# A graph network's last layer: sums transposed by VectorE in 32x32 blocks and put in place by transfers

## The chip, the core and the metric

The kernel runs on one core of a Trainium2 chip. The metric is the device time of one execution in microseconds (us). Before the change the median of three runs is 3499.28 us (3495.52 to 3499.89). A core has five engines that run their own instruction streams: TensorE (PE, with its weight loads shown apart as PEld), VectorE (DVE), ScalarE (ACT), GpSimd (POOL) and SyncE (SP). In this kernel SP only issues transfers; POOL and ACT issue some too. Sixteen DMA engines carry them out. Matmuls write to PSUM, eight banks of 2 KB for each of 128 partitions; the other engines work on PSUM and on the larger SBUF; transfers move data between SBUF and DRAM.

## The reference, cut to what matters

Four layers run on the same 3327 nodes with 512 features and one adjacency matrix. Each adds its result to its input and normalises the rows. The change touches the last one, an attention with 4 heads of 128 features:

```python
h = (x @ W).reshape(N, 4, 128).transpose(1, 0, 2)
si, sj = einsum('hnd,d->hn', h, a1), einsum('hnd,d->hn', h, a2)
e = leaky_relu(si[:, :, None] + sj[:, None, :], 0.2)
attn = softmax(where(adj > 0, e, -9e15), axis=-1)
y = elu(einsum('hij,hjd->hid', attn, h).transpose(1, 0, 2).reshape(N, 512))
x = layernorm(x + y)
```

## The kernel before

**Layout.** The nodes are padded to 26 tiles of 128 (`NT`), and split into two halves of 13 tiles, 1664 columns (`HALF`, `IW`). The attention layers (0, 2 and 3; layer 1 is a mean over neighbours) share the class `Layer`. `attention` (L478) runs eight units: two halves of target nodes by four slots `s`. In layers 0 and 2 a slot is two heads of 64 features (`HS` = 2), in the last layer, called L3, one head of 128 (`HS` = 1).

**One unit** (`unit`, L345) loops over the 26 tiles j of source nodes.

- L391: every second j, SP issues the load of `vj`, the scaled features of two tiles (128 KB). The pool has four buffers, so a load waits until PE has done with the fourth pair before it.
- L396: DVE makes `t`, 128x1664, the larger of two factors times the mask. The pool has three buffers in L3: DVE can be at most three j ahead of PE.
- L399: ACT makes `y`, a step function of `t`, in fp8.
- L405: PE adds `vj` transposed times `t` into the four PSUM banks `po`, which hold the unit's sums with features on partitions and nodes along the columns (`CUTS`: 448, 448, 384 and 384 columns). An f32 product shows as two rows of the trace.
- L365 (`den`): every second j, PE adds the products of `y` to the two banks `pd`, which hold denominators. In slot 0 there are twice as many.

**The end of a unit.** `po` has one set of banks, so the next unit's first products wait until the sums are out. DVE copies the first bank to `ob` in SBUF (L423), ACT the other three (L421). Then features must go from partitions to columns: `transposed` (L426) has PE transpose 128x128 blocks of `ob`, four at a time, into a bank `pt` (L429). That makes 13 transposes in four blocks. Without `final`, DVE (in L3) or ACT (elsewhere) copies `pt` to `hb` (L437, L435) and SP stores it to the DRAM tensor `hd` (L438). In half 1 of L3, `final` (L851) takes `pt`: in slots 0 and 1 DVE copies it to `g` in SBUF (L854); in slots 2 and 3 it goes through division, elu and addition at once, and in slot 3 into the statistics. At the end of slot 3 of half 0, and of slots 1, 2 and 3 of half 1, `pd` is copied too (L452, L453), and PE and DVE make the reciprocals `rec` (L455).

**Order.** `unit` returns the transposing steps as a list of jobs. The next unit takes one after each j (L410): two empty ones, then a block, an empty one, a block and so on. So PE does the transposes of one unit inside the next. A second list, `aside` (L801, `later`), gives further steps, one per j, in half 1: while slots 0 to 2 run, the rows of half 0 are loaded from `hd` (L126), divided (L180), put through elu (L185, L191, L192), normalised (L152 to L161) and stored to the output (L133). In slot 2 the first two slots of `g` are divided (L838, on DVE) and go through elu (L841, L846, L847); in slot 3 their statistics follow (L823). PE's order is that of the program. The order of DVE, ACT, POOL and SP is set by a scheduler that places instructions by modelled times and by dependencies.

Of the kernel before, what the change touches and what calls it, by code (L numbers as in the profile page):

```python
# [18 lines left out]
P = 128  # L19
# [13 lines left out]
def kernel(  # L33
# [10 lines left out]
    nc = tc.nc  # L44
# [6 lines left out]
    HALF = NT // 2  # L51
    FW = F // 2
    assert F == 512 and NT % 2 == 0 and N < NP and NT < 32
    IW = HALF * P
# [5 lines left out]
    QUADS = [(s, min(4, HALF - s)) for s in range(0, HALF, 4)]  # L60
# [53 lines left out]
    hd = dram.tile([NP, F], F32, name="hd")  # L114
# [108 lines left out]
    class Layer:  # L223
# [121 lines left out]
        def unit(self, pools, half, s, background, aside, final=None, ending=None):  # L345
            H, D, HS = self.H, self.D, self.HS
            tp, yp, vp, rp, sp, po_p = pools
            i0 = half * IW
# [6 lines left out]
            po = [po_p.tile([P, 512], F32, name=f"po{c}") for c in range(4)]  # L355
# [60 lines left out]
            den(NT - 2, late)  # L416

            ob = sp.tile([P, IW], F32, name="ob", bufs=1)
            for c, (a_, z) in enumerate(CUTS):
                if c:  # L420
                    nc.scalar.copy(ob[:, a_:z], po[c][:, :z - a_])  # L421
                else:
                    nc.vector.tensor_copy(ob[:, a_:z], po[c][:, :z - a_])  # L423
            t0 = half * HALF

            def transposed(s0, n):  # L426
                pt = qp.tile([P, 4, P], F32, name="pt", tag="q")
                for q in range(n):
                    nc.tensor.transpose(pt[:, q, :], ob[:, (s0 + q) * P:(s0 + q + 1) * P], ident)  # L429
                if final:  # L430
                    final(s, s0, n, pt)
                    return
                hb = sp.tile([P, 4, P], F32, name="hb")
                if HS == 2:
                    nc.scalar.copy(hb[:, :n], pt[:, :n])  # L435
                else:
                    nc.vector.tensor_copy(hb[:, :n], pt[:, :n])  # L437
                nc.sync.dma_start(out=hd[(t0 + s0) * P:(t0 + s0 + n) * P, s * P:(s + 1) * P]  # L438
                                  .rearrange("(t p) f -> p t f", p=P), in_=hb[:, :n])

            nothing = lambda: None
            jobs = [nothing, nothing]
            for s0, n in QUADS:
                jobs += [lambda s0=s0, n=n: transposed(s0, n), nothing]
            if s < NS - 1 and not (final and s > 0):
                return jobs

# [307 lines left out]
    def third(first):  # L755
        with tc.tile_pool(name="col3", bufs=1) as cp:
# [33 lines left out]
            with tc.tile_pool(name="f3", bufs=2) as fp, tc.tile_pool(name="f4", bufs=1) as gp:  # L790
                g = gp.tile([P, HALF, F], F32, name="g")
# [59 lines left out]
                def final(s, q0, n, pt):  # L851
                    qs = slice(q0, q0 + n)
                    if s < 2:
                        nc.vector.tensor_copy(g[:, qs, s * P:(s + 1) * P], pt[:, :n])  # L854
                        return
                    h = fp.tile([P, 4, P], F32, name="h", bufs=2)
                    nc.vector.tensor_tensor(h[:, :n], pt[:, :n], rec[:, HALF + q0:HALF + q0 + n, s:s + 1]
                                            .to_broadcast([P, n, P]), op=ALU.mult)
                    e = fp.tile([P, 4, P], F32, name="e")
                    nc.scalar.activation(e[:, :n], h[:, :n], AF.Exp)  # L860
                    y = g[:, qs, s * P:(s + 1) * P]
                    nc.vector.scalar_tensor_tensor(y, e[:, :n], 1.0, y, op0=ALU.min, op1=ALU.add)
                    nc.vector.scalar_tensor_tensor(y, h[:, :n], 0.0, y, op0=ALU.max, op1=ALU.add)
                    if s == NS - 1:
                        for q in range(q0, q0 + n):
                            nc.vector.bn_stats(out=st[:, q, 1, :], in_=g[:, q, FB:])
                            nc.vector.bn_aggr(out=mv[:, q, :], in_=st[:, q, :, :])

                L3.attention(lambda pool, half, s: [lambda: L3.prepare(fp, 1, "xr", 2), lambda: L3.cut(fp, 1, "e", 2)]
                             if (half, s) == (0, 0) else [], later=later, final=final)  # L870
                cut_ = min(8, HALF)
                for qs in (slice(0, cut_), slice(cut_, HALF)):
# [158 lines left out]
```

## Time and profile before

| | |
|---|---|
| median of three runs | 3499.28 us |
| the profiled execution | 3489.1 us |
| its span, first to last instruction | 3486.7 us |
| L3's attention, first product of its loop to last | 2766.9 to 3460 us of the span |
| 2786 to 3369: PE busy | 582.3 of 583.2 us |
| the same stretch: DVE, ACT busy | 413.0 and 402.2 us |
| mean granted clock of PE | 0.983 |
| one transpose (L429) | 273 ns |
| one t product (L396) | 1947 ns |
| one ob copy by DVE (L423), 128x448 | 617 ns |
| one pt copy by DVE (L437), 128x512 | 684 ns |

A line of the order of time gives the start, the length, the engine, the line of the kernel, the operation, output<-inputs, partitions x columns, and how many instructions are merged in it; in brackets the idle time before it and what ended that. Times inside the span are counted from its first instruction.

### The profile page before, as it was taken

The numbers are of one execution on the slowest core, as the hardware profiler recorded it, in microseconds if no ns is written. First come the engines' busy times: TensorE is split into PE (matmuls) and PEld (weight loads), VectorE is DVE, ScalarE is ACT, GpSimd is POOL, SyncE is SP. The second block draws the span as 40 slices with busy tenths as digits, with TensorE's granted clock in tenths as the row PEclk, the third lists the DMA queues.
The fourth block names the chain that finished last, engine by engine and source line by source line (L and its number), as shares of the span: only waits on it lengthen the run. The fifth ranks groups of instructions, "written<-read, shape, count | busy, mean of one in ns | idle before, by whom it ended". The sixth has DMA issues, their size and how long they took to land.

```text
span 3486.7 us, 48120 instructions
## 1 busy us (share of the span) xinstructions
PE 3325.6 (95%) x18873; PEld 1701.2 (49%) x18926; DVE 2694.9 (77%) x2759; ACT 2396.6 (69%) x2336; POOL 181.2 (5%) x289
## 2 busy tenths in 40 slices
PE   6899999999989999999998999999998999999997
PEld 5644444444444455555553444444446754555553
DVE  5599999999967644434439999999998756668886
ACT  1388989899953343433428999899998655558885
POOL 1000000000000111111110000000001000000000
PEclk9999999999999999999999999999999999999998
DMA  9535211101133432222221111111116511112211
GB/s 352 179 104 161 67 44 41 54 27 51 37 105 125 131 90 73 70 61 75 73 66 35 48 47 48 47 46 46 29 39 197 183 33 44 40 46 91 81 38 47
DMA packets 208452, 276.65 MB, mean 79 GB/s; under 512 B 19321, under 2 KB 140355, under 8 KB 208228
## 3 DMA queue, kind: packets, MB, share of 16 engines
q1 hardware_dynamic: 173622, 157.37, 14.1%
q0 software_dynamic: 22736, 89.80, 8.3%
q10 hardware_dynamic: 11870, 26.42, 2.4%
q8 instruction: 149, 2.44, 0.3%
q14 instruction: 75, 0.61, 0.1%
HBM read 204.92 MB, written 68.60 MB: 78 GB/s over the span
## 4 chain that ended last, share of the span: by engine, by line
PE 62%; issue 24%; DVE 6%; DMA 5%; ACT 3%; POOL 1%; POOLq 0%; DVEq 0%; SPq 0%; ACTq 0%
PE po L405 34%; PE acc L728 9%; PE pw L264 5%; PE pd L365 5%; DVE t L396 3%; PE pz L617 2%; PE pi L620 2%; DMA raw<-in_adjT_dram 2%; ACT y L399 1%; DMA cy<-ctd 1%; PE pt L429 1%; PE pk L696 1%; PE pt L253 1%; DVE kt L700 1%; PE pe L460 1%
## 5 line engine op out<-in xcount | busy, mean ns | idle before, releaser
L396 DVE SCALAR_TENSOR_TENSOR t<-rb,qc,mask 128x1664 f32<-128x1664 f32 x1040 | 1960.1, 1947 | 200.8 <-PE po L405 158.6
L399 ACT ACTIVATE y<-t,bi,sc 128x1664 fp8e4<-128x1664 f32 x1040 | 1771.7, 1766 | 341.4 <-PE pd L365 317.4
L405 PE MATMUL po<-t,vj 128*64 128x448 f32 (+3 forms) x8320 | 1939.5, 522 | 26.0 <-DVE t L396 24.6
L405 PEld LDWEIGHTS po<-t,vj 128*64 128x64 f32 (+1 forms) x8320 | 857.8, 148 | 977.7 <-issue 681.1
L728 PE MATMUL acc<-zs,kt 128*128 128x512 bf16 x1314 | 396.6, 381 | 1.9 <-issue 0.4
L264 PE MATMUL pw<-wsb,xT 128*128 128x264 f32 (+1 forms) x1248 | 299.3, 395 | 21.7 <-DVE vt L270 19.5
L688 ACT CAST pk<-cy 128x256 f32<-128x256 bf16 x338 | 124.0, 374 | 272.7 <-DVE kt L700 224.8
L728 PEld LDWEIGHTS <-kt 128*128 128x128 fp8e4 x2028 | 198.8, 98 | 229.6 <-issue 34.5
L264 PEld LDWEIGHTS pw<-wsb,xT 128*128 128x128 f32 x1248 | 238.9, 196 | 65.6 <-issue 18.8
L365 PE MATMUL pd<-y,sden 128*32 128x448 fp8e4 (+1 forms) x4160 | 259.8, 342 | 10.5 <-ACT y L399 10.5
L700 DVE SCALAR_TENSOR_TENSOR kt<-pk,mask 128x256 fp8e4<-128x256 f32 x338 | 140.9, 421 | 159.5 <-PE pk L696 158.9
L728 PE MATMUL acc<-zl,kt 128*128 128x512 bf16 x661 | 252.1, 381 | 1.1 <-DMA zl<-zd 0.5
L365 PEld LDWEIGHTS <-sden 128*32 128x32 bf16 x4160 | 117.8, 96 | 162.4 <-issue 139.8
L270 DVE TENSOR_TENSOR vt<-pw,dc 128x256 f32<-128x256 f32 x156 | 59.1, 418 | 98.1 <-ACT dc L265 93.5
L696 PE MATMUL pk<-mask,upto 128*128 128x256 fp8e4 x338 | 92.5, 274 | 21.1 <-ACT pk L688 20.0
L353 POOL DMA_DIRECT2D rb<-r x40 | 21.5, 539 | 1646.8 <-DVE t L396 1610.1
L268 ACT COPY fc<-pw 128x8 f32<-128x8 f32 (+1 forms) x156 | 22.8, 163 | 112.1 <-PE pw L264 101.8
L617 PE MATMUL pz<-wn,xT 128*128 128x512 f32 x208 | 95.0, 600 | 1.2 <-ACT xT L611 1.2
L620 PE MATMUL pi<-wl,xT 128*128 128x512 f32 x208 | 93.5, 592 | 0.0
L590 POOL DMA_DIRECT2D cy<-ctd x91 | 67.8, 745 | 400.2 <-ACT pk L688 273.5
L708 DVE SCALAR_TENSOR_TENSOR y<-acc,cnt,bnb 128x512 f32<-128x512 f32 x26 | 19.5, 751 | 85.1 <-PE acc L728 85.1
L524 DVE TENSOR_SCALAR mask<-raw 128x832 fp8e4<-128x832 int32 (+2 forms) x86 | 50.2, 592 | 45.0 <-DMA raw<-in_adjT_dram 44.4
(165 smaller groups left out, 1732.2 us busy)
## 6 DMA issues: line engine op xcount, KB each, us to landing
vj<-v SPq DMA_DIRECT2D x312, 128.0 KB
rb<-r POOLq DMA_DIRECT2D x40, 832.0 KB, 4.7
cy<-ctd POOLq DMA_DIRECT2D x78, 256.0 KB, 3.9
v<-vt SPq DMA_DIRECT2D x75, 256.0 KB
h<-hd SPq DMA_DIRECT2D x65, 256.0 KB
raw<-in_adjT_dram ACTq DMA_DIRECT2D x38, 416.0 KB
raw<-in_adjT_dram SPq DMA_DIRECT2D x37, 416.0 KB
hd<-hb SPq DMA_DIRECT2D x60, 256.0 KB
```

Source lines behind the costliest of these rows:

```text
L264: nc.tensor.matmul(pw[e][:, :FW + H], xT[:, c, :], wsb[:, c, e, :], start=c == 0, stop=c == FC - 1)
L365: nc.tensor.matmul(pd[c][32 * kk:32 * kk + 32, :w_], lhsT, rhs, start=(kk, c) not in seen, skip_group_check=final is not None, stop=last a ...
L396: nc.vector.scalar_tensor_tensor(t, rb[k], self.qc[:, j, h:h + 1], mask[:, j, i0:i0 + IW], op0=ALU.max, op1=ALU.mult)
L399: nc.scalar.activation(y, t, AF.Sigmoid, bias=self.bi[:, j, h:h + 1], scale=self.sc[:, j, h:h + 1], saturate=False)
L405: nc.tensor.matmul(po[c][k * D:(k + 1) * D, :z - a_], vj[:, j % 2, k * D:(k + 1) * D], ts[k][:, a_:z], start=j == 0, stop=j == NT - 1)
L590: nc.gpsimd.dma_start(out=cy[:, :n, :], in_=ctd[t:t + n, b * GW:(b + 1) * GW] .rearrange("(o t) i -> o t i", o=1).to_broadcast([P, n, GW]))
L617: nc.tensor.matmul(pz, xT[:, c, :], wn[:, c, :], start=c == 0, stop=c == FC - 1)
L620: nc.tensor.matmul(pi, xT[:, c, :], wl[:, c, :], start=c == 0, stop=c == FC - 1)
L688: nc.scalar.copy(pks[k % 2], carry[b, t // 4 * 4][:, t % 4, :])
L696: nc.tensor.matmul(pk, upto, mask[:, t, i0:i0 + GW], start=False, stop=True, skip_group_check=True)
L700: nc.vector.scalar_tensor_tensor(kt, pk, NEIGHBOURS, mask[:, t, i0:i0 + GW], op0=ALU.is_le, op1=ALU.mult, saturate=False)
L728: nc.tensor.matmul(acc, kts[t][:, s * P:(s + 1) * P], zs[:, t, c, :] if c < 2 else zl[:, t, :], start=t == 0 and c == 0, stop=t == NT - 1 ...
```

## The change

In L3 alone, in all units but slots 2 and 3 of half 1 (`by_dma`):

- DVE takes all four banks of `po` to `ob`, each with a transpose that works on squares of 32x32: within a square, rows and columns change places; the squares stay where they are. ACT has none of these copies.
- PE's 13 transposes, the copies out of `pt` and the stores of `hb` are gone from these units. Right after the four DVE transposes SP issues four transfers to `hd`, one for each group of 32 partitions. Each writes 32 features of 1664 nodes, in runs of 32 numbers (128 bytes), 1664 runs to a transfer.
- In half 1, slots 0 and 1, a job of the next unit (after its third j for slot 0, its fourth for slot 1) has SP load `g` from `hd`, in place of the DVE copies.

```diff
             ob = sp.tile([P, IW], F32, name="ob", bufs=1)
+            by_dma = HS == 1 and not (final and s > 1)
             for c, (a_, z) in enumerate(CUTS):
-                if c:
+                if by_dma:
+
+                    nc.vector.transpose(ob[:, a_:z], po[c][:, :z - a_])
+                elif c:
                     nc.scalar.copy(ob[:, a_:z], po[c][:, :z - a_])
                 else:
                     nc.vector.tensor_copy(ob[:, a_:z], po[c][:, :z - a_])
...
                 hb = sp.tile([P, 4, P], F32, name="hb")
-                if HS == 2:
-                    nc.scalar.copy(hb[:, :n], pt[:, :n])
-                else:
-                    nc.vector.tensor_copy(hb[:, :n], pt[:, :n])
+                nc.scalar.copy(hb[:, :n], pt[:, :n])
...
-            for s0, n in QUADS:
-                jobs += [lambda s0=s0, n=n: transposed(s0, n), nothing]
+            if by_dma:
+                for b in range(4):
+                    nc.sync.dma_start(out=hd[i0:i0 + IW, s * P + 32 * b:s * P + 32 * b + 32]
+                                      .rearrange("(q i) f -> i q f", i=32),
+                                      in_=ob[32 * b:32 * b + 32, :].rearrange("p (q f) -> p q f", f=32))
+                if final:
+                    jobs.append(lambda: final(s, 0, HALF, None))
+            else:
+                for s0, n in QUADS:
+                    jobs += [lambda s0=s0, n=n: transposed(s0, n), nothing]
...
                     if s < 2:
-                        nc.vector.tensor_copy(g[:, qs, s * P:(s + 1) * P], pt[:, :n])
+                        nc.sync.dma_start(out=g[:, qs, s * P:(s + 1) * P], in_=hd[HALF * P:, s * P:(s + 1) * P]
+                                          .rearrange("(q p) f -> p q f", p=P))
                         return
```

## The prediction, made before the changed kernel was run

> **What bounds the kernel now.** I read the busy times first, then the windows of the last layer, then its order of time on TensorE.
>
> ```profile
> PE 3325.6 (95%) x18873; PEld 1701.2 (49%) x18926; DVE 2694.9 (77%) x2759; ACT 2396.6 (69%) x2336; POOL 181.2 (5%) x289
> ```
>
> ```profile
> 2900.00:3000.00 100.00, 100.00 (x388) 50.19 (x386) 63.83 (x37) 55.79 (x35) 0.53 (x1) 1.00 0.13 38
> 3200.00:3300.00 100.00, 99.08 (x414) 51.41 (x407) 78.16 (x78) 87.41 (x72) 4.17 (x8) 1.00 0.27 84
> ```
>
> PE leads, but its share of the whole span would prove little. The windows of the changed stage (columns: stretch, its length, busy us of PE, PEld, DVE, ACT, POOL, clock, DMA share, GB/s) show PE without a gap while VectorE has 36 us of 100 free in half 0 and 22 in half 1. A busy PE need not be a PE at its peak, so I take the price of the transposes from the rhythm of the stream, not from their own durations. Half 0, slot 1, with and without a block of four transposes:
>
> ```profile
> 2872.58 0.56 PE L365 MATMUL pd<-y,sden 128*32 128x448 fp8e4 x8
> 2873.07 3.06 PE L405 MATMUL po<-t,vj 128*128 128x448 f32 x8
> 2875.96 0.60 PE L429 MATMUL pt<-ident,ob 128*128 128x128 f32 x4
> 2876.40 2.96 PE L405 MATMUL po<-t,vj 128*128 128x448 f32 x8
> 2879.29 0.56 PE L365 MATMUL pd<-y,sden 128*32 128x448 fp8e4 x8
> ...
> 2892.39 0.56 PE L365 MATMUL pd<-y,sden 128*32 128x448 fp8e4 x8
> 2892.88 5.86 PE L405 MATMUL po<-t,vj 128*128 128x448 f32 x16
> 2898.66 0.56 PE L365 MATMUL pd<-y,sden 128*32 128x448 fp8e4 x8
> ```
>
> From one pd group to the next (two values of j, a "pair") is 6.71 us with the block and 6.27 without. Four transposes cost the stream 0.44 us, 0.11 each, not the 0.273 that one lasts.
>
> **What goes from PE.** Six units lose 13 transposes each. They ran inside the following unit. In the four that are followed by slots 1, 2, 3 of half 0 and slot 1 of half 1: 3 x 0.44 + 0.12 (6.39 - 6.27, the single one) = 1.44 each, 5.8 together. Slot 0 of half 1 has pairs of 7.04 and 6.72 against 6.65: 3 x 0.39 + 0.07 = 1.24. Slot 2 of half 1 has 6.67 and 6.34 against 6.27: 1.27. Sum **8.3 us**, all on the path as long as nothing new stops PE.
>
> **What goes from the others.** ACT loses three ob copies per unit (3 x 0.478), DVE one ob copy (0.617) and the four copies out of pt (3 x 0.684 + 0.283). Neither bounds the stage; I count nothing.
>
> **What DVE gets: four transposes per unit.** The trace has no DVE transpose. Nearest row: the ob copy from the same PSUM bank, 128x448 in 0.617; 64 columns fewer at the slope of the pt copies ((683 - 283) ns / 384 columns) give 0.55. The four: 2.33 us. Upper end: a DVE operation that is slow per element, the reciprocal, 0.471 for 52 columns and 0.799 for 104, 6.3 ns a column: 2.8 and 2.4, together 10.5 us. Below the copy there is no reason to go. I take 2.33, since both move every element once. [...]
>
> Whether 2.33 is hidden is settled at the boundary of two units, here slot 1 to slot 2 of half 0:
>
> ```profile
> 2939.95 1.95 DVE L396 SCALAR_TENSOR_TENSOR t<-rb,qc,mask 128x1664 f32<-128x1664 f32 x1 [1.54 <-PE po L405]
> 2941.82 0.62 DVE L423 COPY ob<-po 128x448 f32<-128x448 f32 x1
> 2942.57 0.94 PE L365 MATMUL pd<-y,sden 128*32 128x448 fp8e4 x16
> 2942.68 0.48 ACT L421 COPY ob<-po 128x384 f32<-128x384 f32 x1 [0.17 <-PE po L405]
> 2943.44 4.89 PE L405 MATMUL po<-t,vj 128*128 128x448 f32 x13
> ```
>
> In the changed program's instruction order the transposes stand where the one copy stood, after the t of j=0 and j=1 of the next unit. So PE has 5.8 us of work in hand and DVE starts at 2941.8. PE wants the four banks back at 2943.44, 2944.2, 2945.0 and 2945.7; DVE is done with the last at 2944.15. The t of j=2, queued behind, is ready at 2946.1 and wanted at 2949.2. Cost nothing; the four may take 3.85 us before PE waits. After slot 0 the limit is 4.6, as the double set of pd products fills PE until 2860.77. At slot 0 to 1 of half 1 a t product now stands between the first and second transposes: 3197.2 + 0.62 + 1.87 + 1.7 = 3201.4, wanted by 3203.0. Nothing.
>
> Slot 1 to 2 of half 1 is different:
>
> ```profile
> 3279.96 1.95 DVE L396 SCALAR_TENSOR_TENSOR t<-rb,qc,mask 128x1664 f32<-128x1664 f32 x1 [0.33 <-PE po L405]
> 3281.83 0.69 DVE L191 SCALAR_TENSOR_TENSOR xr<-e,xr 128x512 f32<-128x512 f32 x1
> 3284.22 0.54 PE L365 MATMUL pd<-y,sden 128*32 128x448 fp8e4 x6 [0.92 <-ACT y L399]
> ```
>
> The scheduler now puts between that t (j=1) and the next: L180, L191, transpose, L192, L191, transpose, L192, two transposes, two db copies, two statistics, one aggregate. With 0.68 for each 512-column step (0.60 where they overlap): first transpose done 3283.7, second 3285.7, last 3287.5, next t (j=2) 3292.0. PE wants the banks from 3283.8: it waits 1.15 for the second, 0.45 for the third, and 0.8 for the t of j=2. That is 2.4, and the 0.92 that it waits there for ACT today falls inside it: **1.5 us lost**. Bounds: -0.9 (today's wait goes, none comes) to 4 (the e of L185 late too).
>
> At slot 2 to 3 the copy of the first bank now stands ahead of the t of j=0 and j=1. That t is ready 3.4 us after j=25 began, wanted after 2.89 + 0.87 = 3.8. Nothing, margin 0.4.
>
> **The transfers.** Each unit issues four scatters of 1664 packets of 128 B, 416 packets per DMA engine, in place of three of 512 and one of 128 packets of 512 B; two loads of g (1664 packets of 512 B) come new.
>
> ```profile
> q1 hardware_dynamic: 6045, 2.93, 10.1%
> ...
> hd<-hb SPq DMA_DIRECT2D x3, 256.0 KB
> ```
>
> In 2900 to 3000 a packet of 485 B took 0.101 x 100 x 16 / 6045 = 26.7 ns of an engine. For 128 B the lower end is by bytes, 7 ns. The upper end is 31, from the one row of tiny packets: the cb load, 3328 packets of 2 B, 208 per engine, landed 6.5 us after issue. I take 26.7: 11.1 us per unit.
>
> On SP's queue the scatters wait for the fourth transpose. In the changed order four vj loads of the next unit stand ahead of them; queued behind is its fifth, which PE releases 6.3 us into that unit and wants at 25.1. Landing takes 2.4 (the 128 KB xr load's), so the scatters must drain within 22 us, 53 ns a packet. Twice my price is hidden.
>
> [...]
>
> In half 1 the load of g waits on SP for the scatters to land. For slot 1: 3287.5 + 11.1 + 2.4, then 104 x 26.7 ns + 2.4: about 3306. DVE's first product on it (L838) now stands behind the t of j=10, which waits for PE to end j=7 at about 3314. Hidden by 8 us; without that cover DVE would hold PE up once the two t in hand, 6 us, are used.
>
> **Sum.** 8.3 - 1.5 = 6.8 us. The profiled execution took 3489.1 (span 3486.7 and 2.4 around it): it would be 3482.3. The shown runs have median 3499.28, 10 us above; I take the same 6.8 off it: **3492.5**. That is 0.19%, while 0.2% (7 us) is about what a measurement of this kernel can tell from no change. So the forecast lies on that line.
>
> **Rivals.** (1) No loss at the boundaries: L180 and L191 run earlier than I place them, ACT without its copies is in time. For it: 138 of DVE's waits in this stage are for PE. Against: DVE has least room there. 8.3 to 9.2 off: 3490 to 3491. (2) Half 1 gives most back: the scheduler's new order puts the t products late at slots 1 to 2 and 2 to 3, 3 to 6 us in all: 3495 to 3498, no change. (3) Slower, by the rate of the DVE transpose. Place: each boundary; price: whatever the four take over 3.85 us (4.6 after slot 0). At 10.5 us: 5.9 + 3 x 6.7 in plain boundaries, 6.5 and 10 in the two of half 1, 42 us: 3534. It decides from about 4.9 us for the four, where the six boundaries eat the 6.8. Against it: the copy row. (4) Slower, by the scatters: above 53 ns a packet the vj loads starve PE; at 65 ns 416 x 12 ns = 5 us in six units, 30 us: 3522. (5) It doesn't do what it says: PE is paced by something else and the freed slots stay empty: no change. Against: PE has no gap in 2900 to 3000.
>
> **Chances.** Forecast (4.5 to 8 off) 0.49, half of it beyond 7 us; (1) 0.20; (2) 0.13; (3) 0.08; (4) 0.07; (5) 0.03. Faster by over 0.2%: 0.245 + 0.20 = 0.45. Within: 0.245 + 0.13 + 0.03 = 0.40. Slower: 0.15. Range: 3486 is 9.2 off and 4 for the spread of the shown runs below their median; 3508 takes in (2) and the mild parts of (3) and (4), whose bounds beyond are left out with about 1 in 10.
>
> **What would show it.** Pairs of 6.27 us throughout slots 1 to 3 of half 0; no wait of po for DVE at those boundaries; the four transposes 2.3 us; a wait of 1 to 3 us of po or of t near slot 1 to 2 of half 1; the scatters about 27 ns a packet; no wait of po for a vj load. A transpose near 1.2 us, po waiting for DMA, or L838 waiting for g would prove me wrong.

## The result, and the profile after it

The changed kernel takes 3498.73 us (median of four runs, 3494.16 to 3503.11); the kernel before, with one more run of it, 3497.40 (four, 3491.38 to 3499.89). The ratio is 1.0006, 95% interval 0.9986 to 1.0026. Twelve further runs of the changed kernel beside 24 of the kernel before gave 1.0006 again, 0.9997 to 1.0016. So there is no gain: the forecast of 3492.5 is 6.2 us too low, and the time lies inside its range. The profiled execution of after took 3494.16, span 3492.0. The trace of before is of an execution of 3489.1 us, 8.3 below that kernel's median, that of after 4.6 below its own: sums from one trace are not medians.

The busy times hide the story: PE is busy for 3.3 us less, at the same share of the span.

```profile
PE 3322.3 (95%) x18795; PEld 1696.4 (49%) x18848; DVE 2690.0 (77%) x2753; ACT 2387.5 (68%) x2318; POOL 181.2 (5%) x289
```

The windows of the stage, with the columns explained ahead of the prediction, show that the two halves part ways. In half 0 PE is still without a gap. In half 1 it is idle for 3.3 of 100 us (before: 0.9), and its granted clock is 0.97.

```profile
2900.00:3000.00 100.00, 100.00 (x386) 49.49 (x385) 64.29 (x37) 54.99 (x33) 0.53 (x1) 1.00 0.16 39
3200.00:3300.00 100.00, 96.74 (x372) 48.98 (x371) 77.05 (x79) 81.43 (x66) 4.17 (x8) 0.97 0.40 111
```

In half 0 the rhythm is what was forecast. PE's order of time in slot 1, where blocks of four transposes stood: from one pd group to the next is 6.28 us, and no L433 (the transposes' line now) lies between.

```profile
2867.80 6.07 PE L405 MATMUL po<-t,vj 128*128 128x384 f32 x17
2873.80 0.56 PE L365 MATMUL pd<-y,sden 128*32 128x448 fp8e4 x8
2874.29 5.86 PE L405 MATMUL po<-t,vj 128*128 128x448 f32 x16
2880.08 0.56 PE L365 MATMUL pd<-y,sden 128*32 128x448 fp8e4 x8
```

VectorE's order at the boundary of slots 1 and 2 of half 0: the four transposes take 2.10 us in all, and the t behind them is not late.

```profile
2942.06 2.10 DVE L423 STREAM_TRANSPOSE ob<-po 128x448 f32<-128x448 f32 x4
2944.08 1.91 DVE L396 SCALAR_TENSOR_TENSOR t<-rb,qc,mask 128x1664 f32<-128x1664 f32 x1
```

**Where the gain went** is seen when the stage is cut into slots. A slot is counted from its first po product to the next slot's, the last one to the reciprocal products at the end; each start is read in PE's order of time. Slot 0 of half 0 is left out: counted from 2776.4, behind the products L304, it takes 84.4 us before and 85.7 after, and at its start the granted clock is 0.50 for 3.4 us before and for 6.8 after.

| us | half 0, slots 1 to 3, each | half 1: slot 0 | slot 1 | slot 2 | slot 3 | sum |
|---|---|---|---|---|---|---|
| before | 82.67 | 91.99 | 83.93 | 85.38 | 86.55 | 595.85 |
| after | 81.24 | 89.06 | 84.11 | 93.51 | 89.56 | 599.96 |
| after, a second execution | 81.24 | 90.75 | 84.12 | 93.50 | 89.89 | 601.97 |

Four slots are shorter; slots 1 to 3 of half 1 give it all back. PE's waits in after, from slot 0 on, name two places (before had 0.9 us for y at slot 1 to 2; 1.1 for db at the very end is in both):

```profile
PE pd L365 <- ACT y L399: 4.5, 1, 4.5
PE po L405 <- DVE ob L423: 3.3, 2, 2.8
```

**First place, slot 1 to 2 of half 1.** All engines in order of time:

```profile
3274.95 0.69 DVE L180 TENSOR_TENSOR h<-h,rec 128x512 f32<-128x512 f32 x1 [3.53 <-DMA h<-hd]
3275.56 1.95 DVE L396 SCALAR_TENSOR_TENSOR t<-rb,qc,mask 128x1664 f32<-128x1664 f32 x1
...
3278.63 0.64 DVE L423 STREAM_TRANSPOSE ob<-po 128x448 f32<-128x448 f32 x1
...
3279.32 1.28 PE L405 MATMUL po<-t,vj 128*128 128x448 f32 x2 [2.81 <-DVE ob L423]
...
3280.36 0.64 DVE L423 STREAM_TRANSPOSE ob<-po 128x448 f32<-128x448 f32 x1
...
3281.06 1.86 PE L405 MATMUL po<-t,vj 128*128 128x448 f32 x2 [0.45 <-DVE ob L423]
```

The last line's bracket names the transpose, but the transpose is not slow. Read upwards: VectorE sat idle for 3.53 us in L180, the first of the rows' last steps (divide a row of half 0), because the row's load had only been issued at 3269.88, on SP's queue behind a load of vj, and took about 5 us to land, beside an 832 KB load of rb issued at 3268.93. The scatters are not in it: from 3266 to 3276 only 96 packets are under 512 B. The scheduler had put that L180 ahead of the t of j=1, and the transposes stand behind that t.

**Second place, slot 2 to 3.** Again all engines:

```profile
3363.73 3.44 ACT L399 ACTIVATE y<-t,bi,sc 128x1664 fp8e4<-128x1664 f32 x2
...
3367.19 1.28 ACT L850 ACT_TABLE_LOAD   x1
...
3368.48 0.42 ACT L850 ACTIVATE e<-g 128x256 f32<-128x256 f32 x1
3368.91 1.28 ACT L399 ACT_TABLE_LOAD   x1
...
3370.21 1.77 ACT L399 ACTIVATE y<-t,bi,sc 128x1664 fp8e4<-128x1664 f32 x1
...
3372.03 0.86 PE L365 MATMUL pd<-y,sden 128*32 128x448 fp8e4 x6 [4.46 <-ACT y L399]
```

In after a table load of 1.28 us stands ahead of each exp of g and another ahead of the y behind it, so with an exp of 128x512 (0.63) a pair of j costs ACT 1.28 + 0.63 + 1.28 + 3.44 = 6.63 us where PE needs 6.27. ACT falls behind while elu lasts and catches up when it is over. The exps of g started between 3319.7 and 3357.5 before; now they start between 3328.3 and 3368.5, up to the boundary, although slot 2 begins 5.4 us earlier, and the y of j=25 is 4.5 us late.

**And the clock.** Windows in after (the clock is the third number from the end): behind each of the two waits, and after the reciprocal products L469 in slots 2 and 3, the granted clock is 0.50 for 3.41 us. Between these windows it is 1.00.

```profile
3279.95:3283.36 3.41, 2.96 (x6) 1.13 (x5) 3.38 (x7) 3.40 (x5) 1.28 (x2) 0.50 0.27 84
3283.36:3293.61 10.25, 10.25 (x49) 6.93 (x48) 8.00 (x12) 7.64 (x7) 0.20 (x1) 1.00 0.65 109
3293.61:3297.02 3.41, 3.41 (x7) 1.61 (x5) 1.84 (x3) 1.20 (x2) 0.00 (x0) 0.50 0.54 182
...
3372.11:3375.52 3.41, 3.41 (x10) 1.50 (x10) 2.89 (x3) 3.41 (x6) 0.00 (x0) 0.50 0.00 0
...
3385.76:3389.18 3.42, 3.42 (x6) 1.58 (x5) 0.48 (x3) 0.00 (x0) 0.15 (x1) 0.50 0.00 0
```

The price shows in groups of equal work: eight po products after L469 take 3.04 us, or 4.74 in such a stretch; the first 24 of a slot take 8.65, or 9.97 after the second wait. A busy window at 0.50 loses half of its 3.41 us, 1.7.

### The profile page after: what moved, and what is told of

The parts are those of the page before. It is cut to its first block, busy times and chain, and to the rows that moved or that the text cites. A ratio compares the mean times of both kernels' runs of the same rounds, so it can differ in the third digit from the quotient of the medians.

```text
span 3492.0 us, 47945 instructions
## 1 busy us (share of the span) xinstructions
PE 3322.3 (95%) x18795; PEld 1696.4 (49%) x18848; DVE 2690.0 (77%) x2753; ACT 2387.5 (68%) x2318; POOL 181.2 (5%) x289
## 4 chain that ended last, share of the span: by engine, by line
PE 60%; issue 24%; DVE 6%; DMA 6%; ACT 3%; POOL 1%; SPq 0%; POOLq 0%; DVEq 0%; ACTq 0%
PE po L405 34%; PE acc L737 9%; PE pd L365 5%; PE pw L264 4%; DVE t L396 3%; PE pz L626 3%; PE pi L629 2%; DMA raw<-in_adjT_dram 2%; ACT y L399 1%; DMA cy<-ctd 1%; PE pk L705 1%; DVE kt L709 1%; PE pe L469 1%; PE pt L433 1%; PE pt L253 1%
```

## Experiments

Theory A: the transposes do leave the path, and the two places in half 1, both made by the new order of steps, give the gain back. The rivals: scatters or VectorE transposes cost what they replace (B, C), the second wait has another cause (D). Where an expectation speaks of "the stage" it has slot 0 of half 0 in it; 84.4 us less, or 85.6 where it starts from the full change's 685.6, gives the sums here. Sums are one execution each, ratios are medians of 4 to 12 runs against 24 to 35 of the kernel before.

**Half 0 alone** (the copies out of pt as in the kernel before).

```diff
-            by_dma = HS == 1 and not (final and s > 1)
+            by_dma = HS == 1 and not final
```

> Only the four units of half 0 go through VectorE transposes and scatters; all of half 1 is as before. Measure: the stage from the first product of L3's loop to the reciprocal products at its end, 680.3 us before and 685.6 after the full change. Theory A (the transposes do leave the path, and the loss sits at two boundaries of half 1): slots 1 to 3 of half 0 and slot 0 of half 1 run 3 x 1.43 + 1.24 = 5.5 us shorter and nothing is given back, stage 674 to 676, time about 5 us below before. Rival B (scatters and VectorE transposes cost about as much as the TensorE transposes): three of five units with them are in, so the stage stays at 680 or above.

Measured: 3492.16 us, ratio 0.9989 (0.9980 to 0.9997): 3.5 us gained. Slots 1 to 3 of half 0 take 81.24 each, so B falls, although the whole stage stayed above 680, as B had it: the rest is given back in half 1. "Nothing is given back" was wrong: the rows' steps were scheduled anew here too, PE waits 1.78 us for y at slot 1 to 2 (0.92 before), and slots 0, 2 and 3 of half 1 have slower stretches of 1.7 to 3.3 us; the sum is 597.83.

**Half 0 and slot 0 of half 1.**

```diff
-            by_dma = HS == 1 and not (final and s > 1)
+            by_dma = HS == 1 and not (final and s > 0)
```

> As the one with half 0 alone, and slot 0 of half 1 too; slot 1 of half 1 is as before. Theory A says that the loss at slot 1 to 2 of half 1 is not the price of VectorE's transposes there (there are none in this kernel) but of the order of the rows' last steps: in this program L180, which waits for a late load of h, again stands between the t products of j=0 and j=1. So: 674 to 676, less 1.4 for slot 1's pairs, plus 3 to 6 for a wait of 2 to 3 us and the lower clock behind it, 676 to 680, and no wait at slot 2 to 3. Rival C (the transposes at that boundary are what costs): no wait there, 673 to 674.

Measured: 3487.27 us, ratio 0.9975 (0.9966 to 0.9985); sum 592.24, expected 591.6 to 595.6. The copies out of pt are as in the kernel before. The wait is there although the bank is copied, not transposed:

```profile
3272.64 0.69 DVE L180 TENSOR_TENSOR h<-h,rec 128x512 f32<-128x512 f32 x1 [3.59 <-DMA h<-hd]
...
3276.98 4.23 PE L405 MATMUL po<-t,vj 128*128 128x448 f32 x7 [2.84 <-DVE ob L427]
```

C falls: the first place is the order's. No wait stands at slot 2 to 3, where the elu steps end earlier in this program.

**Elu of g four j earlier.**

```diff
                     elif s == 2:
-                        jobs += [none] * 4
+                        jobs += [none] * 0
```

> The full change, and the four empty jobs ahead of the elu steps of g in slot 2 of half 1 are gone, so that the steps stand four j earlier in the program; nothing else. Theory A: the wait of 4.5 us for y at slot 2 to 3 is ScalarE falling behind while it does the elu steps to the end of the unit; with four j to catch up it goes, and with it 1 to 3 us of lower clock behind it: stage 685.6 - 5.5 to 7.5 = 678 to 680. Rival D (TensorE waits there for another cause, the scatters' traffic or the copy of the first bank that stands ahead of t): no change, 685 to 686.

Measured: 3493.40 us, ratio 0.9994 (0.9984 to 1.0004). The wait for y is gone, the wait for po is not (2.92 and 0.72). Four waits of 0.35 to 0.42 for t appear inside slot 2; the sum is 595.53, expected 592.4 to 594.4: a miss by 1.1. D falls.

**Everything eight j earlier.** (The expectation's bracket is wrong on one point: the 4 stayed 4. So the elu steps too moved by eight j.)

```diff
                     if s == 0:
-                        jobs += [none] * 12
+                        jobs += [none] * 4
```

> The full change, with the rows' last steps in half 1 eight j earlier and the elu steps of g four j earlier still (12 and 4 empty jobs become 4 and none). In this program the four transposes at slot 1 to 2 of half 1 stand closer together, with L180 still once ahead of the t product of j=1. Theory A: the wait at slot 2 to 3 goes (5.5 to 7.5 us), that at slot 1 to 2 goes too if that L180 finds its row loaded (3 to 6 us): stage 672 to 677 if both, 678 to 680 if one. Rival B or D: 684 to 686.

Measured: 3489.55 us, ratio 0.9978 (0.9969 to 0.9988); sum 586.64. Both waits are gone and no slower stretch is left in these slots. There is one new wait, 1.63 us for t: from 3311.9 to 3325.3 VectorE makes two t where PE takes four, with eight divisions of g, eleven more steps of g and a wait of 1.02 us for a load between them.

**The same shift in the kernel before.**

```diff
                     if s == 0:
-                        jobs += [none] * 12
+                        jobs += [none] * 4
```

> The kernel before, with the rows' last steps in half 1 eight j earlier (12 empty jobs become 4), as in the shifted kernel that was faster than before. It tells whether that gain is the shift's own. Theory A: before has only one wait inside L3's half 1 (0.92 us for y at slot 1 to 2) and a slower stretch or two behind waits, so the shift alone is worth 0 to 3 us: 3492 to 3496 where before has 3495.7. Rival E (the shift alone is the gain): 3487 to 3490.

Measured: 3495.94 us, ratio 1.0001 (0.9992 to 1.0011); sum 594.59, the wait for y gone. E falls: the shift alone is worth nothing that can be measured; with the change it is worth 9 to 10 us.

**Seven j earlier.**

```diff
                     if s == 0:
-                        jobs += [none] * 12
+                        jobs += [none] * 5
```

> The full change with the rows' last steps seven j earlier (12 empty jobs become 5). In VectorE's order no L180 stands among the transposes of any boundary: at slot 1 to 2 of half 1 they follow the t of j=1 in one run. Theory A: no wait at the three boundaries of half 1; slots 1 to 7 together 584.7 to 588 us against 595.9 before and 600.0 after the full change; time 3486 to 3490. If the boundaries are not the cause: 596 to 600 and 3495 to 3499.

Measured: 3490.50 us, ratio 0.9987 (0.9977 to 0.9996); sum 592.39, a miss. The wait for po is gone, but 0.74 for y appears at slot 0 to 1 and 1.52 for t inside slot 2, and two slower stretches follow L469.

**Each transpose of half 0 made three times.**

```diff
-                    nc.vector.transpose(ob[:, a_:z], po[c][:, :z - a_])
+                    for _ in range(1 if final else 3):
+                        nc.vector.transpose(ob[:, a_:z], po[c][:, :z - a_])
```

> The full change, but in the four units of half 0 each VectorE transpose is made three times over, 12 in place of 4 (6.3 us for 2.1); the values stay. It tries the limit of 3.85 us of the prediction. Theory A: PE waits 6.3 - 3.85 = 2.4 us for po at the ends of slots 1, 2 and 3 and 1.7 at that of slot 0, 8.9 in all, and some 1 to 3 more each for the lower clock behind a wait: slots 1 to 3 then 83.7 to 86.7 us where the full change has 81.24. Rival F (these boundaries have more cover than worked out): below 82.

Measured: 3508.41 us, ratio 1.0038 (1.0024 to 1.0052); slots 1 to 3 take 83.80, 83.79 and 83.79. VectorE's order, then PE's, at one boundary:

```profile
2948.48 6.08 DVE L424 STREAM_TRANSPOSE ob<-po 128x448 f32<-128x448 f32 x12
```

```profile
2951.30 1.77 PE L405 MATMUL po<-t,vj 128*128 128x448 f32 x4 [1.14 <-DVE ob L424]
2954.15 9.94 PE L405 MATMUL po<-t,vj 128*128 128x384 f32 x28 [1.08 <-DVE ob L424]
```

6.08 us of transposes make PE wait 1.14 + 1.08 = 2.22, so 3.86 were covered; the prediction had 3.85. F falls. Waits this short brought no lower clock: the 28 products in 9.94 us go at the pace of 24 in 8.65; the expectation's 1 to 3 us for it was wrong.

**Each scatter of half 0 issued three times** (`hx` holds two spare DRAM tensors).

```diff
-                    nc.sync.dma_start(out=hd[i0:i0 + IW, s * P + 32 * b:s * P + 32 * b + 32]
+                    for dst in [hd] if final else [hd] + hx:
+                        nc.sync.dma_start(out=dst[i0:i0 + IW, s * P + 32 * b:s * P + 32 * b + 32]
```

> The full change, but in half 0 each of the four scatters is issued three times, twice into spare DRAM tensors, 12 in place of 4. Theory A (scatters are hidden): at 13.6 ns a packet 3 x 416 packets are 17 us of every DMA engine, and SP issues for 3 x 4.7 = 14 us; both are below the 22 us after which the next load of vj comes late: slots 1 to 3 stay at 81.24 us. Rival B (the scatters cost): each unit longer by 0.5 us or more, slot 0 of half 1 as well.

Measured: slots 1 to 3 at 81.24, slot 0 of half 1 at 90.75, as in the second execution of after; 3500.54 us, ratio 1.0012 (1.0002 to 1.0021), not apart from the full change's own interval. A window of 22 us from a slot's start, first in after, then here (packets, MB, share of 16 engines):

```profile
q1 hardware_dynamic: 7808, 1.38, 34.0%
```

```profile
q1 hardware_dynamic: 20775, 2.86, 82.4%
```

In after, 6784 of the packets are short; the other 1024 at 26.7 ns take 27 of 0.34 x 22 x 16 = 120 us, so a 128 B packet takes 13.6 ns. Three times that traffic stays hidden.

**The change once more,** unaltered.

> The full change once more, unaltered, for more runs of it beside the kernel before, and for a second profile. Theory A: the two waits of half 1 stand where they stood (2.8 + 0.5 us for po, 4.5 us for y), slots 1 to 3 of half 0 at 81.24 us; the slower stretches behind waits and behind the reciprocal products may fall elsewhere. Time 3494 to 3499. Rival G (the waits are an accident of one execution): the waits are gone or at other places.

Measured: 3499.54 us, ratio 1.0006 (0.9997 to 1.0016). The waits stand where they stood: 2.81 and 0.72 for po, 4.46 for y. G falls.

**Rows eight j earlier, elu left at its place.**

```diff
                     if s == 0:
-                        jobs += [none] * 12
+                        jobs += [none] * 4
...
                     elif s == 2:
-                        jobs += [none] * 4
+                        jobs += [none] * 12
```

> The full change; the rows' last steps in half 1 eight j earlier, but the elu steps of g left at their place in the program (12 and 4 empty jobs become 4 and 12). It takes the first wait alone. Theory A: no wait for po at slot 1 to 2 of half 1, as L180 finds its row loaded; the elu steps of g, which VectorE's order has now up to j=24 in place of up to j=1 of the next unit, leave a wait of 1 to 4.5 us for y at slot 2 to 3. Slots 1 to 7 together 588 to 594 us, time 3490 to 3494. Rival C (the wait for po is the price of VectorE's transposes there): it stays.

Measured: 3485.81 us, ratio 0.9967 (0.9953 to 0.9980), sum 588.01. The wait for po is gone, with four transposes in place; L180 finds its row loaded. The shift leaves one row's steps at this boundary where after has two, so no run tells how much of the wait is the late load and how much the steps among the transposes. VectorE's order:

```profile
3272.51 0.68 DVE L180 TENSOR_TENSOR h<-h,rec 128x512 f32<-128x512 f32 x1
3274.13 1.95 DVE L396 SCALAR_TENSOR_TENSOR t<-rb,qc,mask 128x1664 f32<-128x1664 f32 x1 [0.94 <-PE po L405]
3276.00 1.17 DVE L423 STREAM_TRANSPOSE ob<-po 128x448 f32<-128x448 f32 x2
```

The expected wait for y was a miss: there is none. ACT's order shows why: the last exp of g starts at 3349.21, 12 us ahead of the boundary, and at 3355.21 ACT already waits for PE.

```profile
3349.21 0.42 ACT L850 ACTIVATE e<-g 128x256 f32<-128x256 f32 x1
3349.64 1.28 ACT L399 ACT_TABLE_LOAD   x1
3350.94 3.44 ACT L399 ACTIVATE y<-t,bi,sc 128x1664 fp8e4<-128x1664 f32 x2
3355.21 3.44 ACT L399 ACTIVATE y<-t,bi,sc 128x1664 fp8e4<-128x1664 f32 x2 [0.84 <-PE pd L365]
```

**Both.**

```diff
                     if s == 0:
-                        jobs += [none] * 12
+                        jobs += [none] * 4
...
                     elif s == 2:
-                        jobs += [none] * 4
+                        jobs += [none] * 8
```

> The full change with 4 and 8 empty jobs in place of 12 and 4: rows eight j earlier, elu steps of g four j earlier, and in VectorE's order no more than four divisions of g ahead of a t product (eight stood there where the shifted kernel waited 1.6 us). Theory A: no wait at any boundary nor inside slot 2, slots 1 to 7 together 584.7 to 587 us, time 3486 to 3490, the fastest with VectorE's transposes in six units.

Measured: 3488.52 us, ratio 0.9975 (0.9966 to 0.9984). No wait in any slot; the sum is 588.43 all the same, above the 584.7 to 587 expected, for two slower stretches at L469 (1.7 and 2.1 us).

**Slot 2 of half 1 too** (on top of the last; after four more empty jobs, its jobs load h by quads).

```diff
-            by_dma = HS == 1 and not (final and s > 1)
+            by_dma = HS == 1 and not (final and s > 2)
...
                     h = fp.tile([P, 4, P], F32, name="h", bufs=2)
+                    if pt is None:
+                        nc.sync.dma_start(out=h[:, :n], in_=hd[(HALF + q0) * P:(HALF + q0 + n) * P, s * P:(s + 1) * P]
+                                          .rearrange("(q p) f -> p q f", p=P))
...
```

> As the one with 4 and 8 empty jobs, and slot 2 of half 1 goes through VectorE and the scatters too: its sums are loaded from DRAM into h, four tiles at a time, in place of 13 more TensorE transposes. Theory A: slot 3's pairs with transposes fall from 6.67 to 6.27, 1.27 us in all, and four transposes at slot 2 to 3 stay inside the cover: slots 1 to 7 together 583.5 to 586 us, time 3485 to 3489. If four transposes at that boundary cost a wait: 585 to 589 us.

Measured: 3484.24 us (median of six), ratio 0.9959 (0.9943 to 0.9974), the lowest median here, 11.7 us below the kernel before. Slot 3's pairs are 6.27 us. The sum is 587.74, expected 583.5 to 586, with slower stretches at two of the groups of reciprocal products. PE's waits from slot 1 of half 0 on:

```profile
PE pe L473 <- DVE db L466: 1.1, 1, 1.1
PE po L405 <- DVE t L396: 0.6, 2, 0.4
```

## Why the prediction was right in its parts and wrong in its sum

- **8.3 us off PE: right.** Take each slot without waits and at full clock: 81.24 three times, 89.06, 81.24 (e.g. both shifted kernels), 84.14 (rows only) and 86.55 make 584.7. For before: 82.67 three times, 91.99 - 1.62 (eight po products in 4.66 for 3.04), 82.67 (its shifted version), 85.38, 86.55: 593.0. The difference is 8.3. Rival 5 is out.
- **2.33 us for the transposes and a cover of 3.85: right**, at 2.10 and 3.86. Rival 3 named the point from which it would turn slower, and the tripled transposes went past it.
- **Slot 0 to 1 of half 1, nothing lost: right.** The full change has no wait there.
- **Slot 1 to 2, "1.5 us lost": the step failed.** The steps from the t of j=1 on were listed rightly, but that t was taken at the time that it has in before. The L180 that now stands ahead of it is not in the walk, and it waited 3.53 us for its row. PE's wait is 3.3 us in place of 2.4, for the banks alone, with slower clock on top.
- **Slot 2 to 3, "Nothing, margin 0.4": the step that failed most.** It followed t and not y. The same new order pushed the elu steps of g to the end of the unit, and ACT, which was counted as not bounding, delivered the y of j=25 4.5 us late.
- **The price of a wait** was taken as its length. In after, slots 1 to 3 of half 1 are 15.2 us above their floor, and 7.9 of that are waits; four windows at half clock make 6.8 more. In before the same slots and the one ahead are 2.9 above: 0.9 of waits, and 1.7 for one window. In the second execution of after they are 17.3 above: 8.2 of waits, 8.5 for five windows. So floor, waits and windows give each of the three sums to within 0.6 us.
- **Scatters: hidden, as said, for a price twice too high**: 13.6 ns a packet, not 26.7. Rival 4 is out; three times the traffic is hidden too. No division waits for the load of g.

Rival 1, no loss at the boundaries, is out with the two waits. Rival 2, at 0.13, named both places and "no change", though with 3 to 6 us and for late t products. The runs show 7.7 us of waits, for banks and for y, and lower clock behind them. That the measured time lies in the range is owed to the room left for this rival, not to the path that the forecast took. The sum of it: 8.3 gained; 7.0 us more of waits; and the two windows at half clock behind them, which all four traces with both waits have, 3.4. If the windows behind L469 come equally often in both kernels, after should be 2.1 us slower. The medians say 1.3 and 3.6, and both intervals of the ratio take in 1. How often the windows behind L469 come in executions without a trace is not known. Nor is the order among the kernels from 0.9959 to 0.9978, whose intervals overlap.

## What to carry to other kernels

Work taken off the bounding engine is gained only if the engines beside it still deliver at the boundaries; when a scheduler sets their order, an edit moves steps that it doesn't touch, so go through the new order for every input that the bounding engine waits for, with each step's own inputs (was its load issued in time?). When a large saving gives nothing, cut the stage into units of equal work: the units that gained and those that gave back stand apart at once. Then shift the side work before giving the change up: here two counts of empty jobs turned no change into a gain of 0.2 to 0.3%.

## What the runs showed of the hardware

- **A wait can cost more than its length.** Behind PE waits of 2.8 and 4.5 us in after the granted clock was 0.50 for 3.41 us. Behind one of 1.78 us in the run with half 0 alone, 24 po products took 10.34 us in place of 8.65. Behind 0.92 us in before the clock stayed at 1.00, and behind 1.63 us in the run with everything eight j earlier too: 16 products in 5.85 us, as without a wait. But in before it was 0.50 for 6.8 us after a wait of 1.09 us that the last reciprocal products follow, so the length alone doesn't tell. An estimate from the 0.50 and the 3.41 us: a busy window at half clock loses 1.7 us. The measured 4.74 - 3.04 and 10.34 - 8.65 are 1.7 too.
- **A group of tiny products can do the same with no idle time.** After the 26 products of 8 columns (L469) the next eight po products take 3.04 us in some executions and 4.4 to 5.9 in others, of one and the same kernel too. What differs is where the group falls. In these traces the granted clock changes only at the edges of a grid of 3.41 us (in after 3279.95, 3283.36, 3293.61, 3297.02 and so on). Half 1 has three such groups a trace, 42 in the 14 traces: in 23 at least 2.28 us of the group lies between two neighbouring edges, and the clock is 0.50 in the next window; in the other 19 it is 2.26 us at most, and the clock stays at 1.00. Two executions of after, slot 0 of half 1: in the first the edge at 3116.11 (48 windows before 3279.95) cuts the group into halves of 1.48 us; in the second 2.54 us lie between 3118.44 and 3121.85, and the clock is 0.50 from there to 3125.26.

```profile
3114.63 2.96 PE L469 MATMUL pe<-c1w,db 128*128 128x8 f32 x26
3117.45 3.04 PE L405 MATMUL po<-t,vj 128*128 128x448 f32 x8
```

```profile
3118.01 2.96 PE L469 MATMUL pe<-c1w,db 128*128 128x8 f32 x26
3120.83 4.74 PE L405 MATMUL po<-t,vj 128*128 128x448 f32 x8
```

- **Issuing a scatter held SP.** A transfer of 1664 runs of 128 B kept SP for 0.32 to 2.7 us, the four below for 4.67; the load of vj ahead of them took 0.36. SP's order in after:

```profile
2942.91 0.36 SPq L391 DMA_DIRECT2D vj<-v  x1
2944.19 4.67 SPq L446 DMA_DIRECT2D hd<-ob  x4
```

- **Short packets.** 128 B took 13.6 ns (after, the 22 us from a slot's start), 485 B in the mean took 26.7 (before, 2900 to 3000): half the price a packet, twice the price a byte (0.106 to 0.055 ns).
